# Where the heads of the last two slots and of the half slots are made in a graph layer with routed experts

## The chip, the cores and the metric

The kernel runs on one core of a Trainium2 chip. The metric is the device time of one execution in microseconds; the median of three runs before the change is 528.12 us. A core has a matrix engine (PE, with its weight loads shown apart as PEld), a vector engine (DVE), a scalar engine (ACT), a general engine (POOL, which here issues all indirect transfers) and a queue that issues plain transfers (SP).

## What is computed

The input is a table x of 2048 nodes with 256 features. The first half adds to each row a weighted sum of normalised neighbour rows over 67,584 edges. The second half, in which the change lies, is a layer of eight experts of which every row uses its two best:

```python
x = x + _L0_gnn_ref(_layernorm(x, axis=-1), edge_weight, edge_index, node_vec1)
x = x + _L0_ffn_ref(_layernorm(x, axis=-1)[None], ...)[0]
...
weights = top_p / top_p.sum(axis=-1, keepdims=True)
h = gelu(einsum('end,edh->enh', xe, W1) + b1)
y = einsum('enh,ehd->end', h, W2) + b2
out = (weights[:, :, None] * sel).sum(axis=1)
```

D is 256, the hidden width H is 1024, and all arithmetic here is in 32-bit floats.

## The kernel before

Only rows that chose an expert are computed for it. The rows of an expert are cut into **slots**: a whole slot has two tiles of 128 rows, a half slot has one (an expert with an odd number of tiles has one half slot). Which expert a slot belongs to, and which rows it holds, is known only on the chip. With this data 16 whole slots and 2 half slots run: `whole[0]` to `whole[13]`, two more whole slots set aside as `finals`, and `halves[0]` and `halves[1]`. Of them `whole[0]` to `whole[9]` and `finals` exist for any data; `whole[10]` on and all of `halves` stand in nested branches on the two counts `n_whole` and `n_half` (lines 1053 to 1063). A queue that finds a branch not taken goes through its other arm, where POOL waits for its outstanding transfers.

A slot has these steps:

- `load_slot` (L859) finds the slot's row numbers on DVE (L865 to L871, which end by writing the tile `to_i`), issues four loads on SP (scale columns `ec` L843, first weights L844, second weights L845, bias row `b` L846), and gathers the slot's rows `xs` with one indirect transfer per tile on POOL (L850).
- `head` (L876) transposes the rows on PE into the PSUM tile `px` (L883, four transposes for a whole slot, two for a half), scales them into `xeT` on DVE (L892), finds the rows' routing weights on DVE (L902 to L905) and multiplies the bias row by them on ACT (L907, one instruction per tile). `px` has one buffer.
- `layer_1` (L909) runs eight chunks `c`: two products on PE into `ph` (L918; the records count each as two) and a Gelu on ACT (L920). `ph` has three buffers. It has an argument `between` that runs a function ahead of chunk `c`.
- `layer_2` (L924) runs eight products per tile into `py` (L932, two buffers), and DVE makes `ys` (L935).
- `put_y` (L939) adds `ys` to rows of a table in device memory, `y_d`, with an indirect transfer on POOL (L940).

The order on PE, DVE, ACT and SP is written out by hand; POOL's is left to a scheduler. `run_slot(s, nxt, *more)` issues `load_slot` for the slots in `more`, then layer 1 of `s`, then the head of `nxt`, then layer 2 of `s`. A whole slot is loaded two slots ahead, into one of three sets of buffers in turn. The finals and the first two half slots have sets of their own, so each is loaded beside another slot: `finals[0]` in slot 6, `finals[1]` in slot 7, `halves[0]` in slot 8, `halves[1]` in slot 9. The heads of `finals[0]`, `finals[1]` and `halves[0]` are made one after the other behind slot 9 (L1046):

```python
for u in range(3, SURE - 2):
    k = u - (SURE - 2) + len(extra)
    run_slot(whole[u], whole[u + 1], whole[u + 2], *(extra[k:k + 1] if k >= 0 else []))
for s in (*finals, halves[0]):
    head(s)
```

Half slot `u` makes the head of half slot `u + 1` and loads half slot `u + 2`; whether these will run is not known when they are issued. In this data `halves[1]` is the last one that runs, so the head of `halves[2]` and the loads of `halves[2]` and `halves[3]` are not used. `to_i` of `halves[3]` shares its buffer with that of `halves[0]`.

At the end (L1066 to L1075) four plain transfers copy `y_d` to `out` (L1069), the rows of `finals[0]` are gathered from `y_d` (L850, `y_rows`) and added to its bias (L1074), its results are written to `out` (L953), the rows of `finals[1]` are gathered from `out`, and its results are written last.

Of the kernel before, what the change touches and what calls it, by code (L numbers as in the profile page):

```python
# [1 line left out]

# [7 lines left out]
F32 = mybir.dt.float32  # L10
# [11 lines left out]
P = 128  # L22
# [4 lines left out]
def kernel(  # L27
# [31 lines left out]
    N, D = x.shape  # L59
# [18 lines left out]
    SURE = (2 * N // P - NE) // TT  # L78
# [20 lines left out]
    for q in range(4):  # L99
        s = slice(q * NB // 4, (q + 1) * NB // 4)  # L100
# [85 lines left out]
    at = find.tile([P, GQ], F32, name="at")  # L186
# [156 lines left out]
    with tc.manual_schedule(engines=ALL):  # L343
# [29 lines left out]
        for n in range(NH):  # L373
# [20 lines left out]
            g, k = divmod(n - 2 * CB - 1, 2 * CB)  # L394
# [99 lines left out]
    with tc.If(n_used < E):  # L494
# [11 lines left out]
        with tc.tile_pool(name="any", bufs=2) as anyp, tc.tile_pool(  # L506
            name="ps_any", bufs=2, space=PSUM
# [36 lines left out]
    slotp = right("slot", 2)  # L544
# [34 lines left out]
    whole = []  # L579
    for i in range(EARLY + NF):  # L580
        k = i - EARLY if i - EARLY < LAST else i - EARLY + 2
        if k < NF:
            whole.append(Slot(k if i >= EARLY else i, TT, i % len(sets), i % (AHEAD + 2), i % 2,
                              i < EARLY))
    finals = [Slot(LAST + i, TT, 3 + i, AHEAD + 2 + i, 2 + i) for i in range(2)]
    halves = [Slot(NF + i, 1, 5 + i if i < 2 else (i - 2) % 3, AHEAD + 4 + i % 3, 4 + i % 2)
              for i in range(NE)]
    with tc.manual_schedule(engines=ALL - {ET.Pool}):
# [133 lines left out]
        def list_rows(s):  # L722
            in_lo, in_hi = s["in"]
            n = s["n"] * 2
            for m in range(n):
                nc.tensor.matmul(listed[:, s["i"], :], in_lo[:, m, :], in_hi[:, m, :],
                                 start=(m == 0), stop=(m == n - 1))
# [131 lines left out]
        def load_slot(s):  # L859

            e = ds(offs[s.i], 1)
            tk = slotp.tile([P, TT], F32, name="tk")
            for t in range(s.n):
                pick = slotp.tile([P, P], F32, name="pick", bufs=1)
                nc.vector.scalar_tensor_tensor(pick, iota_p, tile_0[:, t, s.i:s.i + 1], lists,  # L865
                                               op0=OP.is_equal, op1=OP.mult,
                                               accum_out=tk[:, t:t + 1])
            to = slotp.tile([P, TT], F32, name="to")
            nc.vector.scalar_tensor_tensor(to[:, :s.n], tk[:, :s.n], 0.5, spare_r[:, :s.n],
                                           op0=OP.is_lt, op1=OP.mult)  # L870
            nc.vector.scalar_tensor_tensor(tos[s.to][:, :s.n], tk[:, :s.n], -1.0, to[:, :s.n],  # L871
                                           op0=OP.add, op1=OP.max)
            get_weights(s, W1[e], cols_d[e], W2[e], b2[e])
            get_rows(s)

        def head(s):  # L876


            xs = sets[s.set][0]
            pt = ps_x.tile([P, KD, TS], F32, name="px")  # L880
            for t in range(s.n):
                for k in range(KD):
                    nc.tensor.transpose(pt[:, k, t * P:(t + 1) * P],  # L883
                                        xs[:, t, k * P:(k + 1) * P], ident)
            scale_rows(s, pt)
            set_weights(s)

        def scale_rows(s, pt):
            ec = sets[s.set][3]
            xeT = heads[s.head][0]  # L890
            for k in range(KD):
                nc.vector.tensor_scalar(xeT[:, k, :], pt[:, k, :s.n * P], ec[:, KH + k:KH + k + 1],  # L892
                                        ec[:, KH + KD + k:KH + KD + k + 1],
                                        op0=OP.mult, op1=OP.add)

        def set_weights(s):

            xs, w1, w2, ec, b2r = sets[s.set]
            xeT, wt, b2w = heads[s.head]
            expert = (iota_p if s.early else slot_e)[:, s.i:s.i + 1]  # L900
            mine = slotp.tile([P, TT, 2], F32, name="mine")[:, :s.n, :]
            nc.vector.tensor_scalar(mine, xs[:, :s.n, D:D + 2], expert, None, op0=OP.is_equal)  # L902
            wr = slotp.tile([P, TT, 2], F32, name="wr")[:, :s.n, :]
            nc.vector.tensor_mul(wr, mine, xs[:, :s.n, D + 2:D + 4])
            nc.vector.tensor_reduce(wt, wr, AX.X, OP.add)  # L905
            for t in range(s.n):
                nc.scalar.activation(b2w[:, t, :], b2r, AF.Copy, scale=wt[:, t:t + 1])  # L907

        def layer_1(s, between={}):  # L909
            xs, w1, w2, ec, b2r = sets[s.set]  # L910
            xeT = heads[s.head][0]
            hT = slotp.tile([P, KH, TS], F32, name="hT")
            for c in range(KH):
                if c in between:
                    between[c]()
                ph = ps_h.tile([P, TS], F32, name="ph")[:, :s.n * P]
                for k in range(KD):
                    nc.tensor.matmul(ph, w1[:, k, c * P:(c + 1) * P], xeT[:, k, :],  # L918
                                     start=(k == 0), stop=(k == KD - 1))
                nc.scalar.activation(hT[:, c, :s.n * P], ph, AF.Gelu, bias=ec[:, c:c + 1],  # L920
                                     scale=1.0)
            return hT

        def layer_2(s, hT, put, between={}):  # L924
            w2 = sets[s.set][2]
            xeT, wt, b2w = heads[s.head]
            for t in range(s.n):
                if t in between:
                    between[t]()
                py = ps_y.tile([P, D], F32, name="py")  # L930
                for c in range(KH):
                    nc.tensor.matmul(py, hT[:, c, t * P:(t + 1) * P], w2[:, c, :],  # L932
                                     start=(c == 0), stop=(c == KH - 1))
                ys = slotp.tile([P, D], F32, name="ys")
                nc.vector.scalar_tensor_tensor(ys, py, wt[:, t:t + 1], b2w[:, t, :], op0=OP.mult,  # L935
                                               op1=OP.add)
                put(s, t, ys)
# [23 lines left out]
            tc.declare_no_dep(st.ins, group=f"last{s.i}", reason="rows are unique in a slot")  # L961
            tc.add_to_no_dep_group(f"last{s.i}", st.ins)

        def run_slot(s, nxt, *more):
            for m in more:
                load_slot(m)
            hT = layer_1(s)
            if nxt is not None:
                head(nxt)
            layer_2(s, hT, put_y)  # L970
# [38 lines left out]
        hT = layer_1(whole[0])  # L1009
# [8 lines left out]
        set_weights(whole[0])  # L1018
        head(whole[1])
        layer_2(whole[0], hT, put_y, {1: lambda: sum_counts(last_b)})  # L1020
        places(last_b)
        enlist(last_b)
        slots(last_b["all"])
        set_shares(last_b)
        hT = layer_1(whole[1], {4: lambda: list_rows(last_b)})
# [5 lines left out]
        load_slot(whole[EARLY])  # L1031
        head(whole[2])
        layer_2(whole[1], hT, put_y)
        run_slot(whole[2], whole[3], whole[4])
        route_s.close()
        more_w = ctx.enter_context(tc.tile_pool(name="more_w", bufs=1, reuse_waits="tile"))
# [4 lines left out]
        nc.vector.memset(y_rows[1], 0.0)  # L1041
        extra = [finals[0], finals[1], halves[0], halves[1]]
        for u in range(3, SURE - 2):
            k = u - (SURE - 2) + len(extra)
            run_slot(whole[u], whole[u + 1], whole[u + 2], *(extra[k:k + 1] if k >= 0 else []))
        for s in (*finals, halves[0]):  # L1046
            head(s)
    _, (n_whole, n_half) = nc.values_load_multi_w_load_instructions(
        slot_i[0:1, NU:NU + 2], min_val=0, max_val=NF,
        skip_runtime_bounds_check_because="the sums of the experts' slots",  # L1050
# [1 line left out]
    at = lambda ss, i: ss[i] if i < len(ss) else None  # L1052
    with ExitStack() as nest:  # L1053
        for u in range(SURE - 2, len(whole)):
            s = whole[u]
            nest.enter_context(tc.If(n_whole > s.i))
            with tc.manual_schedule(engines=ALL - {ET.Pool}):
                run_slot(s, at(whole, u + 1), *whole[u + 2:u + 3])
    with ExitStack() as nest:  # L1059
        for u, s in enumerate(halves):  # L1060
            nest.enter_context(tc.If(n_half > s.i - NF))
            with tc.manual_schedule(engines=ALL - {ET.Pool}):
                run_slot(s, at(halves, u + 1), *halves[u + 2:u + 3])


    with tc.manual_schedule(engines=ALL - {ET.Pool}):  # L1066
# [3 lines left out]
        for f, y, rows, n in zip(finals, y_rows, (y_d, out), (N + TS, N)):  # L1070
            get_rows(f, y, rows, n)
            hT = layer_1(f)
# [27 lines left out]
```

## Time and profile before

| What | Value |
|---|---|
| median of three runs | 528.12 us (527.67 to 530.58) |
| the profiled execution | 529.07 us, span 527.3 us |
| granted PE clock, mean over the span | 0.955 |
| busy: PE, DVE, ACT, POOL | 457.7, 283.6, 191.6, 156.6 us |
| a whole slot in the steady part | 14.25 us |
| first whole slot in a branch (`whole[10]`) begins | 408.61 us |
| first half slot begins | 467.94 us |
| `finals[0]` begins on PE | 489.49 us |

The span runs from the first to the last instruction, and 1.77 us of the execution's time lie outside it. In the timelines below a row is: start, duration, engine, line, operation, tile written and tiles read, count, and in brackets how long the engine had been idle and what released it. An arrow points from what is read to what is written. SPq and POOLq are the queues that issue transfers.

The share of PE is high over the whole span, but the first 260 us (the graph part and the routing) are not touched by the change. The slots fill 260 to 520 us.

### The profile page before, as it was taken

What the parts mean: (1) busy time and instruction counts of PE and PEld (TensorE: products, weight loads), DVE (VectorE), ACT (ScalarE), POOL (GpSimd) and SP (SyncE); (2) the same over time, 40 slices, a digit from 0 to 9 for tenths busy, and PEclk for the clock granted to TensorE, in tenths of its full rate; (3) what the DMA queues carried; (4) which work ended last, traced back from release to release, by engine and by line L of the source; (5) the groups of instructions that cost most, each with busy time, mean ns of one, the idle gap of its engine ahead of it and who ended that gap; (6) DMA issues with size and microseconds to landing.
All of it is one profiled execution on the core that took longest, in us unless ns stands there. A gap on an engine that the chain in (4) does not pass through costs nothing. (4 is left out here: it accounts for less than half of the span.)

```text
span 527.3 us, 12108 instructions
## 1 busy us (share of the span) xinstructions
PE 457.7 (87%) x4998; PEld 393.3 (75%) x4998; DVE 283.6 (54%) x599; ACT 191.6 (36%) x439; POOL 156.6 (30%) x127
## 2 busy tenths in 40 slices
PE   0154889898899999899999999999997999996992
PEld 0043778687688788688887888888886888885881
DVE  5698989899999898217847222232234222221011
ACT  1424877333242412038382333333332333332220
POOL 2504153450603000000242533455443144422222
PEclk9995778999899999999999999999999899998997
DMA  6215776757567468894523996679999567748421
GB/s 205 71 42 146 217 222 217 211 174 247 177 205 216 138 187 234 273 347 156 178 50 82 325 341 180 188 234 356 365 363 360 165 178 193 205 102 284 118 106 39
DMA packets 87604, 106.75 MB, mean 202 GB/s; under 512 B 8640, under 2 KB 77360, under 8 KB 85424
## 3 DMA queue, kind: packets, MB, share of 16 engines
q1 hardware_dynamic: 78032, 90.73, 53.2%
q0 software_dynamic: 8032, 14.04, 11.4%
q10 hardware_dynamic: 1472, 1.06, 0.6%
q8 instruction: 44, 0.72, 0.5%
q14 instruction: 24, 0.20, 0.1%
HBM read 79.78 MB, written 28.14 MB: 205 GB/s over the span
## 5 line engine op out<-in xcount | busy, mean ns | idle before, releaser
L333 PE MATMUL py<-xn_sb,ac 128*128 128x264 f32 x512 | 122.5, 395 | 4.4 <-DMA ac<-ad 2.6
L918 PE MATMUL ph<-xeT,w 128*128 128x256 f32 (+1 forms) x576 | 122.5, 371 | 1.6 <-DVEq L1053 0.7
L932 PE MATMUL py<-w,hT 128*128 128x256 f32 x544 | 121.8, 382 | 0.0
L918 PEld LDWEIGHTS ph<-xeT,w 128*128 128x128 f32 x576 | 105.3, 192 | 16.1 <-issue 2.0
L333 PEld LDWEIGHTS py<-xn_sb,ac 128*128 128x128 f32 x512 | 96.1, 192 | 23.9 <-issue 2.9
L920 ACT ACTIVATE hT<-ph,ec 128x256 f32<-128x256 f32 (+1 forms) x144 | 66.5, 462 | 128.3 <-PE ph L918 75.5
L932 PEld LDWEIGHTS py<-w,hT 128*128 128x128 f32 x544 | 103.0, 192 | 13.5
L940 POOL DMA_INDIRECT y_d<-ys,to_i x30 | 48.9, 1630 | 110.2 <-DVE ys L935 88.7
L292 DVE TENSOR_TENSOR hl<-k,iota_b 128x4096 bf16<-128x4096 bf16 x32 | 73.1, 2285 | 3.4 <-PE pa L319 3.4
L319 PE MATMUL pa<-hl,hr 128*32 128x128 bf16 x3072 | 58.3, 241 | 18.3 <-DVE hr L299 15.9
L319 PEld LDWEIGHTS <-hr 128*32 128x32 bf16 x3072 | 52.0, 108 | 27.2 <-DVE hr L299 17.3
L850 POOL DMA_INDIRECT xs<-xr_d,to_i x40 | 41.7, 1043 | 73.7 <-DVE r L616 43.6
L299 DVE TENSOR_TENSOR hr<-eq,w 128x3072 bf16<-128x3072 bf16 x32 | 56.3, 1758 | 2.0 <-DVE eq L295 0.5
L892 DVE TENSOR_SCALAR xeT<-px,ec 128x256 f32<-128x256 f32 (+1 forms) x40 | 19.1, 519 | 70.6 <-PE px L883 68.6
L935 DVE SCALAR_TENSOR_TENSOR ys<-py,wt,b2w 128x256 f32<-128x256 f32 x34 | 16.3, 483 | 71.8 <-PE py L932 62.2
L322 ACT COPY ar<-pa 128x512 f32<-128x512 f32 x64 | 35.4, 583 | 39.6 <-PE pa L319 35.9
L221 POOL DMA_INDIRECT win_s<-in_src,at_i x8 | 13.7, 1709 | 92.7 <-DVE r L282 88.4
L338 DVE TENSOR_TENSOR acc<-acc,py 128x528 f32<-128x528 f32 x32 | 22.2, 700 | 23.0 <-PE py L333 23.0
L907 ACT ACTIVATE b2w<-b,wt 128x256 f32<-128x256 f32 x37 | 16.8, 500 | 39.6 <-DVE wt L905 36.5
L265 PE MATMUL pk<-ident,f 128*128 128x128 f32 x16 | 4.7, 348 | 20.7 <-DVE f L256 16.1
L295 DVE TENSOR_TENSOR eq<-k,iota_b 128x1024 bf16<-128x1024 bf16 x32 | 21.9, 684 | 0.0
L265 PEld LDWEIGHTS pk<-ident,f 128*128 128x128 f32 x16 | 2.4, 159 | 22.9 <-issue 13.0
(193 smaller groups left out, 312.7 us busy)
## 6 DMA issues: line engine op xcount, KB each, us to landing
w<-in_L_ffn_W SPq DMA_DIRECT2D x44, 1024.0 KB, 9.3
ad<-ar SPq DMA_DIRECT2D x32, 512.0 KB, 4.6
ac<-ad SPq DMA_DIRECT2D x16, 1024.0 KB, 6.0
b<-in_L_ffn_b SPq DMA_DIRECT2D x22, 128.0 KB, 9.7
out<-y_d SPq DMA_DIRECT2D x4, 512.0 KB, 6.6
xr_d<-rec SPq DMA_DIRECT2D x1, 1300.0 KB, 6.7
y_d<-acc SPq DMA_DIRECT2D x1, 1280.0 KB, 6.0
acc<-in_x ACTq DMA_DIRECT2D x2, 512.0 KB, 6.0
```

The costliest lines, as they stand in the source:

```text
L292: nc.vector.tensor_tensor(hl.rearrange("p g (n t) -> p g n t", t=2), two(k2[:, 0], g, P), pair(P), OP.is_equal)
L295: nc.vector.tensor_tensor(eq.rearrange("p g (n t) -> p g n t", t=2), two(k2[:, 1], g, RK), pair(RK), OP.is_equal)
L299: nc.vector.tensor_tensor(hr.rearrange("p g i (n t) -> p (g i) n t", t=2), eq[:, :, None, :].to_broadcast([P, GH, 3, RK]), w[:, :, None, : ...
L319: nc.tensor.matmul(pa[j * RK:(j + 1) * RK, m, :], hr[:, g, i, :], hl[:, g, :], start=(i == 0), stop=(i == 2), tile_position=(0, j * RK))
L322: nc.scalar.copy(ar[:, m0:m0 + 4, :], pa)
L333: nc.tensor.matmul(pa[:, i, :DX], acs[g * CB + c][:, b + i, :], xn_sb[:, g * CB + c, :], start=(c == 0), stop=(c == CB - 1))
L338: nc.vector.tensor_add(acc[:, b:b + 2, :], acc[:, b:b + 2, :], pa[:, :, :DX])
L850: nc.gpsimd.indirect_dma_start(out=(sets[s.set][0] if into is None else into)[:, t, :], out_offset=None, in_=(xr_d if rows is None else ro ...
L918: nc.tensor.matmul(ph, w1[:, k, c * P:(c + 1) * P], xeT[:, k, :], start=(k == 0), stop=(k == KD - 1))
L920: nc.scalar.activation(hT[:, c, :s.n * P], ph, AF.Gelu, bias=ec[:, c:c + 1], scale=1.0)
L932: nc.tensor.matmul(py, hT[:, c, t * P:(t + 1) * P], w2[:, c, :], start=(c == 0), stop=(c == KH - 1))
L940: st = nc.gpsimd.indirect_dma_start(out=y_d[:, :], out_offset=bass.IndirectOffsetOnAxis(ap=tos[s.to][:, t:t + 1], axis=0), in_=ys, in_offs ...
```

## The change

```diff
-                ys = slotp.tile([P, D], F32, name="ys")
+                ys = slotp.tile([P, D], F32, name="ys", bufs=4)
...
-        def run_slot(s, nxt, *more):
+        def run_slot(s, nxt, *more, between={}):
             for m in more:
                 load_slot(m)
-            hT = layer_1(s)
+            hT = layer_1(s, between)
...
         for u in range(3, SURE - 2):
-            k = u - (SURE - 2) + len(extra)
-            run_slot(whole[u], whole[u + 1], whole[u + 2], *(extra[k:k + 1] if k >= 0 else []))
-        for s in (*finals, halves[0]):
-            head(s)
+            k = u - (SURE - 2) + len(extra) + 1
+            run_slot(whole[u], whole[u + 1], whole[u + 2], *(extra[k:k + 1] if k >= 0 else []),
+                     between={4: partial(head, extra[k - 1])} if k > 0 else {})
...
         for u, s in enumerate(halves):
             nest.enter_context(tc.If(n_half > s.i - NF))
             with tc.manual_schedule(engines=ALL - {ET.Pool}):
-                run_slot(s, at(halves, u + 1), *halves[u + 2:u + 3])
+                if u > 1:
+                    head(s)
+                run_slot(s, None, *halves[u + 2:u + 3])
```

In words: the four extra slots are each loaded one slot earlier (in slots 5 to 8), and their heads are made inside slots 6 to 9, ahead of chunk 4 of layer 1. `halves[1]` thus gets its head in slot 9 and no longer in `halves[0]`. No half slot makes the head of the next one; from `halves[2]` on, a half slot makes its own at its start, inside its branch. `ys` has four buffers for two, 1 KB per partition each.

More of the change, by code (lines that the diff above doesn't have):

```diff
@@ L1 @@
 from contextlib import ExitStack
+from functools import partial
 import concourse.bass as bass
```

## The prediction

> **What bounds the kernel now.** I read the chain of waits first. From 478 us to the end it runs through transfers, not through PE:
>
> ```profile
> 478.31 1.59 DMA y_d<-ys,to_i
> 479.90 6.59 issue
> ...
> 486.69 1.07 POOL xs L850
> 487.76 1.77 issue
> ...
> 489.76 5.36 DMA y_d<-ys,to_i
> ...
> 498.36 7.93 DMA out<-y_d
> ```
>
> The reader is to see the two additions to `y_d`: that of `halves[0]` at 478.31, that of `halves[1]` at 489.76. The copy to `out` and the rest follow the second one at fixed distances, so the end moves with it.
>
> Second, the timeline between the two, to learn why the second comes so late:
>
> ```profile
> 475.26 3.73 PE L918 MATMUL ph<-xeT,w 128*128 128x128 f32 x32
> 476.94 1.07 POOL L850 DMA_INDIRECT xs<-xr_d,to_i  x1 [7.22 <-DVE to L869]
> 478.31 1.59 POOL L940 DMA_INDIRECT y_d<-ys,to_i  x1 [0.30 <-issue]
> 483.68 0.69 PE L883 MATMUL px<-ident,xs 128*128 128x128 f32 x2 [4.68 <-DMA xs<-xr_d,to_i]
> 483.95 4.60 PEld L932 LDWEIGHTS py<-w,hT 128*128 128x128 f32 x16
> 485.74 0.16 DVE L871 SCALAR_TENSOR_TENSOR to_i<-tk,to 128x1 int32<-128x1 f32 x1 [8.95 <-DMA y_d<-ys,to_i]
> 486.69 1.07 POOL L850 DMA_INDIRECT xs<-xr_d,to_i  x1 [6.79 <-issue]
> 488.99 0.48 DVE L935 SCALAR_TENSOR_TENSOR ys<-py,wt,b2w 128x256 f32<-128x256 f32 x1 [1.89 <-PE py L932]
> ```
>
> Two waits stand here side by side. PE sits 4.68 us for the gathered rows of `halves[2]`, whose head nobody uses, and layer 2 of `halves[1]` waits behind it. DVE sits 8.95 us at the row numbers of `halves[3]` until the addition of `halves[0]` has landed. PE's wait ends last by little: POOL was free again at 487.76, `ys` came at 488.99.
>
> Third, the windows by slot, for PE further up (columns: window, its length, then busy time and count of PE, PEld, DVE, ACT, POOL, granted clock, DMA share, GB/s):
>
> ```profile
> 390.00:404.25 14.25, 14.25 (x69) 12.50 (x68) 3.96 (x17) 4.69 (x10) 6.33 (x5) 1.00 1.08 361
> 404.25:408.61 4.36, 1.69 (x11) 0.99 (x10) 3.88 (x13) 1.28 (x3) 1.59 (x1) 0.93 1.09 356
> 408.61:424.34 15.73, 15.73 (x68) 13.65 (x69) 3.82 (x17) 5.23 (x12) 3.74 (x3) 0.91 0.54 160
> 424.34:438.59 14.25, 14.25 (x69) 12.55 (x68) 3.36 (x13) 4.69 (x10) 5.34 (x4) 1.00 0.71 194
> ```
>
> The three heads behind slot 9 cost PE 4.36 us, and the slot behind them takes 15.73 for 14.25, with the clock at 0.91. In one-microsecond windows it is 0.50 from 409 to 411 and 1.00 from 412 on.
>
> [...] half clock behind the 4.36 us gap, and again at 484 to 486 behind the 4.68 us wait. [...] the ten transposes in the gap indeed didn't keep the clock up. [...] the additions here took 3.8 to 10.1 us to land (median 6.8)[...].
>
> **The change part by part.** All against the profiled execution (span 527.3, time 529.07 us).
>
> *Heads out of the gap.* Removed: 4.36 us of gap and 1.48 us of slow clock (15.73 − 14.25), together 5.84. The branch on `n_whole` now stands directly behind slot 9. Its cost on PE was hidden; between the last transposes' end (408.23) and the first product (408.61) lay 0.38 us. From below it is nothing, from above about 0.7 (the exit from that nest at 467.94 shows 0.68 us idle); I take 0.4.
>
> *Heads into layer 1.* Four transposes cost PE 0.44 us (slot 7: head at 368.41, next product at 368.85), two cost 0.22 (471.59 to 471.81). More weighs what follows them on ACT. In slot 7, from the transposes it takes 0.64 us to L892 and 3.15 us to the end of L907. Ahead of chunk 4 the transposes start at 4 × 0.864 = 3.46 us into the slot (0.864 is the Gelus' spacing), so L907 ends at 6.61 and the Gelu of chunk 4, queued behind it, at 7.09. Chunk 7 wants its `ph` buffer back at 3.46 + 0.44 + 3 × 0.864 = 6.50: with release it waits some 0.65 us. A whole head thus costs 1.09 us. For a half head (L907 ends about 2.2 us after the transposes, by 471.59 to 473.81) the Gelu of chunk 4 is done at about 6.15 and chunk 7 wants it at 6.27: 0.22 us only. Sum: 2 × 1.09 + 2 × 0.22 = 2.62. From below, without any wait, 1.32; from above, if the slack of the half heads goes too and both waits double, 4.1. The other engines hide it: DVE is busy 4 of 14.25 us per slot.
>
> *Loads one slot earlier.* Each is four SP issues, one or two gathers and the DVE steps; they move past `load_slot` of one whole slot on SP and past two additions on POOL. Nothing is added in total. The DMA engines were full (share 1.07) in slots 7 to 9; now slots 6 to 8 are. The gathers took up to 8.9 us to land and have over 12 now. The bias rows are the tightest: issued 3.05 to 4.89 us into a slot and 11.8 to 13.2 us in landing, they are there 16.3 to 16.8 us after that slot's start; L907 wants them at 14.25 + 5.70 = 19.95. Cost nothing, with 3.2 us to spare; each microsecond beyond would be paid on ACT, then on PE.
>
> *Sum on PE up to `halves[0]`*: 5.84 − 0.4 − 2.62 = 2.82 us earlier. The additions of `whole[13]` move by as much. POOL then waits for their landing before the gather at 476.94, so this gather and the addition of `halves[0]` move by 2.82 too; that `halves[0]` itself loses a head of 0.22 us is hidden by POOL.
>
> *The unused head.* PE's 4.68 us wait, two transposes and 1.2 us of slow clock (4.79 for 3.62 us of the same 16 products in `halves[0]`) go. Late next is DVE's wait: L871 stays ahead of L935 in DVE's queue, and behind it the gather of `halves[3]` stays ahead of the addition of `halves[1]` on POOL. That gather ends at 487.76, the addition could start 0.30 us later (as it does at 478.31), at 488.06; it started at 489.76. So only 1.70 us of the wait are won. PE ends `halves[1]` at about 479.5 and is no longer in the chain.
>
> *`ys` with four buffers.* The wait of 0.42 us for a `ys` buffer in `halves[0]` (PE ended at 475.43, `ys` started at 475.85) lies under POOL's wait: nothing. L871 now carries waits for additions of two slots earlier, 28 us old in the steady part: nothing. Other tiles move in memory; the one early instruction that gains a wait, an iota on POOL at 216.42, is read at 246.64: nothing.
>
> *The end.* PE's finals start 9 us earlier, but `finals[0]` needs the gathered `y_d` rows, and the last bias addition came at 516.60 for transfers, not for PE. PE then stands 1.4 us at `py` and ends `finals[1]` near 510, ahead of that addition near 512. The tail keeps its length.
>
> Sum: 2.82 + 1.70 = 4.52 us. The profiled execution would be 524.6 us; it stands 0.95 above the median of the runs, so on the median 528.12 − 4.5 = 523.6 us.
>
> **The rivals.** *More is won (521.6 us).* The addition of `halves[0]` took 7.3 us to land under the loads of unused half slots, that of `halves[1]` 3.9. If the former lands as fast as 5.3, the end gains 2 more. Against it: these loads are released by the same queues and move along.
>
> *The gain upstream is eaten (526.4 us).* If the in-slot heads and the branch cost as much as the gap did, only the 1.70 us are left. For it speaks that my 2.62 is built from spacings, and that DMA is full there; against it, that its upper end (4.1 + 0.7) is still below 5.84.
>
> *Slower (531.6 us).* Bias rows of the extra slots land after 19.95 us. Then L907 holds the Gelus of chunks 4 to 7, and PE stops in chunk 7. At 2 us too late in each of four slots this costs 8 us: 528.1 − 4.5 + 8. It decides from 3.2 us more than landing takes now, and outweighs the gain from about 4.4. Against it: order and amount on SP stay as they were.
>
> **How the numbers follow.** Forecast 0.60 (522 to 525), more won 0.12, eaten 0.18, slower 0.10. A measurement here tells apart about 0.5%, 2.6 us: faster means below 525.5. Faster: 0.58 + 0.12 + 0.04 = 0.74; same: 0.02 + 0.14 = 0.16; slower 0.10. The range goes from 521.2 (more won) to 527.0 (eaten).
>
> **What would show it.** Right: no gap behind slot 9, `whole[10]` at 14.25 us and full clock; slots 6 and 7 about 1.1 us longer, slots 8 and 9 about 0.2; `halves[0]` starting near 465.1; L871 of `halves[3]` still waiting for the addition of `halves[0]`, near 483; the addition of `halves[1]` 0.3 us behind a gather, near 485.2. Wrong: an idle ACT ahead of L907 put down to `b`, PE idle in chunk 7 for over 1 us, a slow clock inside slots 6 to 10, or a last addition that no longer follows L871.

## The result, and the profile after

The changed kernel takes 525.37 us in the median of 16 runs, against 530.56 us of the kernel before in 16 runs of the same comparison. The ratio is 0.9897 with a 95% interval of 0.9872 to 0.9922: 1.0% faster, which is 5.5 us (the two medians lie 5.2 apart). Executions more than 1.5% above the fastest of their kernel (one of these 16, at 530.02 us) are left out of all ratios. The profiled execution took 521.57 us, with a span of 519.8 us.

Spans of single executions mislead here. The graph part, which the change doesn't touch, takes up to 14 us more or less from one execution to the next: in the traces of this study slot 6 begins between 342.91 and 356.74 us. So I measure from the first product of slot 6 to the end of the span, and cut this stretch at the three points that the prediction used: the start of `halves[0]` on PE, the addition of `halves[0]` to `y_d`, and that of `halves[1]`.

| Kernel (one trace each) | slot 6 to `halves[0]` | to its addition | to the addition of `halves[1]` | to the end | sum |
|---|---|---|---|---|---|
| before | 120.69 | 10.37 | 11.45 | 37.54 | 180.05 |
| after | 117.58 | 10.15 | 10.25 | 36.44 | 174.42 |
| after, a second trace | 117.60 | 8.40 | 10.04 | 37.73 | 173.77 |

The sum is 5.6 and 6.3 us shorter, in keeping with the 5.5 us of the comparison. Four lines of the windows of after show the upper part (columns: window, its length, busy time and count of PE, PEld, DVE, ACT, POOL, granted clock, DMA share, GB/s): slot 6, slot 9, the slot behind it, and a stretch to which I come back.

```profile
345.38:360.77 15.39, 14.96 (x74) 12.85 (x73) 5.89 (x24) 5.28 (x12) 7.32 (x6) 1.00 1.06 356
390.64:405.11 14.47, 14.47 (x72) 12.71 (x71) 4.55 (x18) 4.99 (x11) 5.33 (x4) 1.00 0.82 270
405.11:419.37 14.26, 14.26 (x70) 12.56 (x69) 3.46 (x13) 4.70 (x10) 5.33 (x4) 1.00 0.70 194
...
477.25:481.35 4.10, 0.00 (x2) 0.03 (x1) 0.31 (x2) 0.00 (x0) 0.00 (x0) 0.95 0.95 281
```

The gap of 4.36 us behind slot 9 is gone; `whole[10]` begins at 405.11, at the very end of slot 9, and runs at a granted clock of 1.00. Slots 6 and 7 take 15.39 us each for 14.25, slots 8 and 9 take 14.47 and 14.48. The timeline of after (columns as before):

```profile
345.38 3.62 PE L919 MATMUL ph<-xeT,w 128*128 128x256 f32 x16
348.83 0.60 PE L884 MATMUL px<-ident,xs 128*128 128x128 f32 x4
349.26 2.75 PE L919 MATMUL ph<-xeT,w 128*128 128x256 f32 x12
352.45 1.13 PE L919 MATMUL ph<-xeT,w 128*128 128x256 f32 x4 [0.43 <-ACT hT L921]
...
471.73 1.08 POOL L851 DMA_INDIRECT xs<-xr_d,to_i  x1 [6.99 <-PE ph L919]
473.11 1.59 POOL L941 DMA_INDIRECT y_d<-ys,to_i  x1 [0.30 <-issue]
473.63 3.62 PE L933 MATMUL py<-w,hT 128*128 128x256 f32 x16
481.04 0.16 DVE L872 SCALAR_TENSOR_TENSOR to_i<-tk,to 128x1 int32<-128x1 f32 x1 [9.50 <-DMA y_d<-ys,to_i]
481.35 8.63 PE L919 MATMUL ph<-xeT,w 128*128 128x256 f32 x32 [4.10 <-PEq L1059]
481.99 1.07 POOL L851 DMA_INDIRECT xs<-xr_d,to_i  x1 [7.28 <-issue]
483.36 1.58 POOL L941 DMA_INDIRECT y_d<-ys,to_i  x1 [0.31 <-issue]
...
510.74 0.48 DVE L936 SCALAR_TENSOR_TENSOR ys<-py,wt,b2w 128x256 f32<-128x256 f32 x1 [0.36 <-PE py L933]
```

In slot 6 the reader is to see the four transposes ahead of chunk 4 and the one PE wait in chunk 7, put down to a Gelu. Between the two additions, at 473.11 and 483.36, PE's wait for rows is gone, and what is late next is the wait of DVE (L872) for the addition of `halves[0]`, with the unused gather behind it, as forecast. Two things weren't forecast: PE stands 4.10 us in front of `finals[0]`, put down to its own queue at the branch of L1059 (the last of the four windows above: PE idle, DMA share 0.95), and then runs `finals[0]` at half clock for a while (granted clock 0.50 from 481.35 to 484 us, 1.00 from 485 on; 8.63 us for 7.07). And at the end the last `ys` waits for PE, 0.36 us. The chain of waits of after says the same of the additions:

```profile
473.11 1.59 DMA y_d<-ys,to_i
474.70 7.08 issue
...
481.99 0.34 POOL xs L851
...
483.36 5.59 DMA y_d<-ys,to_i
...
491.34 7.73 DMA out<-y_d
```

### The profile page after: what moved, and what is told of

The parts are those of the page before. It is cut to its first block, busy times and chain, and to the rows that moved or that the text cites. A ratio compares the mean times of both kernels' runs of the same rounds, so it can differ in the third digit from the quotient of the medians.

```text
span 519.8 us, 12093 instructions
## 1 busy us (share of the span) xinstructions
PE 453.8 (87%) x4996; PEld 390.3 (75%) x4996; DVE 282.6 (54%) x594; ACT 190.7 (37%) x438; POOL 154.2 (30%) x127
## 5 line engine op out<-in xcount | busy, mean ns | idle before, releaser
L222 POOL DMA_INDIRECT win_s<-in_src,at_i x8 | 11.6, 1454 | 94.0 <-DVE r L283 89.8
```

## The experiments

Each run has one trace, cut in the same way as above:

| Kernel | slot 6 to `halves[0]` | to its addition | to that of `halves[1]` | to the end | sum | ratio to before |
|---|---|---|---|---|---|---|
| heads in the slots only | 117.36 | 10.78 | 13.11 | 36.74 | 177.99 | 0.9943 (0.9916 to 0.997) |
| unused head only | 120.56 | 11.23 | 10.48 | 36.67 | 178.94 | 0.9969 (0.9947 to 0.9992) |
| late bias | 116.18 | 11.24 | 9.88 | 36.73 | 174.03 | 0.9886 (0.9853 to 0.9918) |
| late bias, again | 116.18 | 11.39 | 10.21 | 36.59 | 174.37 | 0.9867 (0.9801 to 0.9933) |
| four row-number tiles | 117.58 | 11.09 | 8.32 | 38.20 | 175.19 | 0.9872 (0.9845 to 0.9899) |
| two `ys` | 117.62 | 11.30 | 9.81 | 37.63 | 176.36 | 0.9929 (0.9888 to 0.9969) |
| two `ys`, again | 117.56 | 8.15 | 10.40 | 37.18 | 173.29 | 0.996 (0.992 to 1.0001) |
| loads in own branch | 117.54 | 8.07 | 7.03 | 36.96 | 169.60 | 0.9807 (0.9726 to 0.9887) |
| that and late bias | 116.18 | 8.07 | 7.02 | 36.89 | 168.16 | 0.9772 (0.9704 to 0.984) |
| that and late bias, again | 116.18 | 8.07 | 7.02 | 36.99 | 168.26 | 0.98 (0.9731 to 0.9869) |

**The two parts of the change, each alone.** First the changed kernel without its part on half slots: `halves[1]` gets its head behind layer 1 of `halves[0]` again, and the head of `halves[2]` is made though nobody uses it.

```diff
-                      between={4: partial(head, extra[k - 1])} if k > 0 else {})
+                      between={4: partial(head, extra[k - 1])} if 0 < k < 4 else {})
...
-                 if u > 1:
-                     head(s)
-                 run_slot(s, None, *halves[u + 2:u + 3])
+                 run_slot(s, at(halves, u + 1), *halves[u + 2:u + 3])
```

> The change without its half-slot part: heads of the two finals and of halves[0] inside slots 6 to 8, loads one slot earlier, but halves[0] makes the head of halves[1] and halves[1] the unused head of halves[2], as before. Theory (two separate gains): slot 6 to the start of halves[0] takes 117.4 us (120.7 before, 117.6 after; one half head of 0.22 is missing); PE then waits some 4.7 us again for the rows of halves[2], and the addition of halves[1] comes 11 to 11.5 us behind that of halves[0] (10.25 after). In all 3.0 to 4.3 us faster than before. Rival (the gap behind slot 9 was hidden by transfers and only the unused head counted): within 1 us of before.

It is 3.0 us faster than before by the ratio (medians 529.36 and 526.56), and 2.1 us in the traces (180.05 − 177.99). Slot 6 to `halves[0]` took 117.36 us, as expected; the distance between the additions was not the expected 11 to 11.5 us but 13.11. The timeline of this kernel shows why:

```profile
479.96 0.69 PE L884 MATMUL px<-ident,xs 128*128 128x128 f32 x2 [5.54 <-DMA xs<-xr_d,to_i]
480.44 6.01 PE L933 MATMUL py<-w,hT 128*128 128x256 f32 x16
486.49 0.48 DVE L936 SCALAR_TENSOR_TENSOR ys<-py,wt,b2w 128x256 f32<-128x256 f32 x1 [3.18 <-PE py L933]
```

PE waits longer for the unused rows (5.54 us), and the half clock that follows (0.50 from 480 to 483 us) now covers most of layer 2 (6.01 us for 3.62), on which the addition waits.

Then the kernel before with only its unused heads taken away:

```diff
-                 run_slot(s, at(halves, u + 1), *halves[u + 2:u + 3])
+                 if u > 1:
+                     head(s)
+                 run_slot(s, halves[1] if u == 0 else None, *halves[u + 2:u + 3])
```

> The kernel before with only its unused heads taken out: halves[0] makes the head of halves[1], later half slots make their own. Theory: the gap behind slot 9 stays (slot 6 to halves[0] 120.7 us), and the addition of halves[1] follows that of halves[0] by some 10.2 us for 11.45, since the row numbers of halves[3] still wait for it to land; 1.2 to 2.3 us faster than before. Rival (PE's 4.7 us wait was worth its full length): 5 us faster.

The gain is 1.6 us by the ratio and 180.05 − 178.94 = 1.1 in the traces; the additions lie 10.48 us apart. PE stands 4.08 us at the branch here too and takes 8.74 us for layer 1 of `finals[0]` (mean clock 0.66 from 485 to 490 us), so this cost belongs to the taking away of PE's wait, not to the heads in the slots. The two parts alone give 3.0 + 1.6 = 4.6 us by their ratios, the whole 5.5: the difference is within the intervals.

**What a head in a slot is made of.** In the changed kernel the bias rows of the four extra heads are multiplied behind the eight Gelus of the slot instead of ahead of that of chunk 4.

```diff
+        def weigh_bias(s):
+            b2r = sets[s.set][4]
+            _, wt, b2w = heads[s.head]
...
-                      between={4: partial(head, extra[k - 1])} if k > 0 else {})
+                      between={4: partial(head, extra[k - 1], False)} if k > 0 else {},
+                      then=extra[k - 1] if k > 0 else None)
```

> The changed kernel with the bias rows of the in-slot head weighed on ACT behind the eight Gelus of layer 1 instead of between the fourth and fifth. Theory (ACT's queue holds up PE in chunk 7): slots 6 and 7 take 14.69 us each for 15.39, slots 8 and 9 stay at 14.47; 1.4 us faster than the changed kernel. Rival (PE waits for the px bank or for DVE): slots 6 and 7 stay at 15.39, same time.

Slots 6 and 7 took 14.69 us each, slots 8 and 9 14.47. So of the 1.14 us of a whole head 0.70 were the Gelu held up behind the bias rows (forecast 0.65), and 0.44 are the transposes (forecast 0.44). `halves[0]` begins 1.4 us earlier. But the time moved by less than its interval can tell, so I ran it again beside the changed kernel itself on one chip.

> The changed kernel with the bias rows of in-slot heads weighed behind the eight Gelus, again. Theory A (PE sets the time from slot 6 to the first half slot, and the additions move with it): slots 6 and 7 at 14.69 us, and the ratio 0.2 to 0.3% below the changed kernel. Rival B (the additions wait for landings that do not move): same slots, ratio equal to the changed kernel within 0.1%.

> The changed kernel itself, to stand beside the three others on one chip. Both theories: ratio to before about 0.990.

The ratios were 0.9867 and 0.9886 (0.9841 to 0.9932), 0.2% apart and far inside the intervals. The traces say where the 1.4 us went: from `halves[0]` to its addition it took 11.24 and 11.39 us, for 10.15 and 8.40 in the changed kernel. In this stretch POOL waits until the last addition of `whole[13]` has landed, which took 6.99 and 7.14 us here and 5.92 and 4.16 there; the stretch is 4.2 us longer than this landing in all ten traces of kernels that load unused half slots. How long the landing takes goes, over the same ten traces, with the moment at which SP issues the second weights of `halves[2]`, the first unused slot: 1.5 to 1.9 us after the start of `halves[0]` the addition took 6.5 to 7.1 us, at 2.1 us 5.9 to 6.2, and at 2.3 to 2.4 us 3.9 to 4.2. So it looks like a race between the addition and these loads. That it isn't the late bias rows as such is seen from the two traces of the kernel with two `ys` (below): one program, 7.13 us in one and 3.93 in the other. No run moved this issue alone.

**Who holds PE in front of the finals?** Either DVE, whose wait at L872 keeps `ys` of `halves[1]` and with it a PSUM buffer, or the branch itself. In the changed kernel the row numbers of the half slots got four tiles in turn instead of three, so that L872 waits for no addition.

```diff
-     tos = [wpool.tile([P, TT], I32, name=f"to_i{i}") for i in range(AHEAD + 7)]
+     tos = [wpool.tile([P, TT], I32, name=f"to_i{i}") for i in range(AHEAD + 8)]
...
-     halves = [Slot(NF + i, 1, 5 + i if i < 2 else (i - 2) % 3, AHEAD + 4 + i % 3, 4 + i % 2)
+     halves = [Slot(NF + i, 1, 5 + i if i < 2 else (i - 2) % 3, AHEAD + 4 + i % 4, 4 + i % 2)
```

> The changed kernel with four tiles of row numbers for the half slots for three, so that those of halves[3] need not wait for the addition of halves[0]. DVE is then free for ys of halves[1] at about 477.3 us on the scale of the changed kernel's trace (481.15 there), and POOL adds it at about 478 (483.36 there). PE's 4.1 us wait ahead of the finals ends together with DVE's wait in the changed kernel. Theory A (PE's branch is slow by itself, because weights for unused half slots fill the DMA engines): PE's finals still begin about 11 us after the start of halves[1]'s layer 1, at half clock, PE then ends last, and the time is within 1 us of the changed kernel. Theory B (PE's wait hangs on the transfer that DVE waits for): the finals begin about 8 us after that start, and the time falls by 3 to 4.5 us.

The timeline of this kernel:

```profile
474.82 0.48 DVE L936 SCALAR_TENSOR_TENSOR ys<-py,wt,b2w 128x256 f32<-128x256 f32 x1 [4.62 <-PE py L933]
478.68 10.12 PE L919 MATMUL ph<-xeT,w 128*128 128x256 f32 x32 [3.90 <-PEq L1059]
479.90 1.58 POOL L941 DMA_INDIRECT y_d<-ys,to_i  x1 [5.37 <-DMA y_d<-ys,to_i]
...
509.56 0.48 DVE L936 SCALAR_TENSOR_TENSOR ys<-py,wt,b2w 128x256 f32<-128x256 f32 x1 [2.93 <-PE py L933]
```

DVE no longer waits, `ys` is there at 474.82, and PE stands 3.90 us all the same: it is the branch. The addition of `halves[1]` gains less than it might, since POOL lets it wait for the landing of the one before in any case (5.37 us idle), and at the end the last `ys` waits 2.93 us for PE. By the ratios the time is within 1.3 us of the changed kernel: behind DVE's wait stood another one that is only 1.7 to 1.9 us shorter (additions 8.32 us apart for 10.04 and 10.25), and the longer end takes part of that back.

**The loads of half slots that don't run.** In the changed kernel a half slot from `halves[2]` on is loaded at the start of its own branch, so that nothing is loaded for a slot that doesn't run. (With data that needs a third half slot, that slot would wait for its own loads; this wasn't tried.)

```diff
                  if u > 1:
+                     load_slot(s)
                      head(s)
-                 run_slot(s, None, *halves[u + 2:u + 3])
+                 run_slot(s, None)
```

> The changed kernel in which half slots from the third on are loaded inside their own branch, so that nothing is loaded for half slots that do not run. The DMA engines are then nearly idle during the two half slots. T is the start of halves[0] on PE. Theory (PE's wait ahead of the finals is its branch, made slow by the unused loads; the addition of halves[1] waits for that of halves[0] to land): PE's finals begin about T + 15 us at full clock (T + 18.4 in the changed kernel), the additions start near T + 8.2 and T + 15.2 (10.2 and 20.4 there), PE ends last, and the time is 3.5 to 5 us under the changed kernel, ratio to before about 0.981. Rival (the wait is a fixed price of leaving the nest): the finals begin at T + 18 us or later at half clock, and the time falls by 1 us at most.

The ratio is 0.9807; its interval just reaches that of the changed kernel, but the stretch from slot 6 on is 4.2 to 4.8 us shorter than in the two traces of the changed kernel. The timeline of this kernel:

```profile
473.61 1.57 POOL L941 DMA_INDIRECT y_d<-ys,to_i  x1 [6.29 <-DVE ys L936]
480.64 1.55 POOL L941 DMA_INDIRECT y_d<-ys,to_i  x1 [5.46 <-DVEq L1059]
481.09 7.14 PE L919 MATMUL ph<-xeT,w 128*128 128x256 f32 x32 [1.26 <-PEq L1059]
```

Each addition now follows its own `ys`, 7.03 us apart; PE stands 1.26 us at the branch instead of 4.10 and keeps its clock (1.00 from 480 to 485 us). The landings show what the unused loads had cost: the addition of `halves[0]` took 7.3 to 8.1 us to land in all ten traces of kernels that issue these loads, and 3.8 to 3.9 us in the three of kernels that don't (from the start of the addition to its semaphore).

How long the branches of L1059 took is seen in the view by line (columns: queue, operation, count, shortest/median/longest in ns, first and last start), first of after:

```profile
L1059 PEldq COMPARE_BRANCH  x4: 65/132/6528, 462.7 to 481.0; - x4
```

then of the kernel with the loads in their branch, and of the one with the heads in the slots only:

```profile
L1059 PEldq COMPARE_BRANCH  x4: 65/132/3688, 465.3 to 480.7; - x4
...
L1059 PEldq COMPARE_BRANCH  x4: 65/127/3487, 463.1 to 486.6; - x4
```

Three of the four are short in each; the one that leaves the nest takes 6.5, 3.7 and 3.5 us. The third kernel issues the unused loads as well, so the loads alone don't make the branch long. The packets of the DMA queues tell more. The trace marks some of them as "instruction", and those of one queue, q8, are 16 KB each. In after two of them lie inside the long branch (474.25 to 480.78): they start at 475.56 and 478.19. In the other two kernels only one lies inside, and the one ahead of it is there before PE comes to the branch. With the loads in their branch it starts 9.2 us after `halves[0]`, in after 12.6 us, beside other transfers (DMA share 1.04 from 474.96 to 476.96 us); PE comes to the branch at 11.3 us in both. In the kernel with the heads in the slots only it starts late too, at 12.3 us, but PE waits for rows first and comes to the branch at 16.7. So I read the long branch as PE meeting a packet there that the unused loads have held up; no run held it up alone. PE's instructions are the same in after and in the kernel with the loads in their branch. Three things go with these loads: the transfers, DVE's wait at L872 and POOL's unused gather. The four row-number tiles took DVE's wait away alone and brought the additions from 10.25 and 10.04 us apart to 8.32; without all three it is 7.03, and the first addition comes 0.3 and 2.1 us earlier as well.

**Both together.** Loads in their own branch and late bias rows:

> The kernel of the run before with the bias rows of in-slot heads weighed behind the Gelus as well. If the two are separate, 1.4 us less than that run, ratio to before about 0.978; if the end is set by transfers and not by PE's slots, the same as that run.

> Late bias rows and loads of the half slots in their own branches. Theory A (unused loads lengthen the landings and PE's branch): 1.0 to 1.3% below the changed kernel, ratio to before about 0.978. Rival B (the ratio of 0.977 measured earlier came from that chip): equal to the changed kernel within 0.4%.

The ratios are 0.9772 and 0.98, the second beside 0.9886 of the changed kernel on the same chip: 0.9% below it, somewhat less than the 1.0 to 1.3 expected, and with intervals that overlap a little. The stretch from slot 6 on is 5.5 to 6.3 us shorter than in the two traces of the changed kernel. This is the fastest version of the study. That it beats the kernel before, the ratios show; that it beats the changed kernel, the ratios and the traces together. Here the 1.4 us of the late bias rows do arrive: 168.16 and 168.26 against 169.60.

**Two buffers for `ys`.** In the changed kernel, `bufs=4` of `ys` was taken back:

```diff
-                ys = slotp.tile([P, D], F32, name="ys", bufs=4)
+                ys = slotp.tile([P, D], F32, name="ys")
```

> The changed kernel with two ys buffers as before. Theory (the wait for a ys buffer lies under POOL's wait): slot lengths and the distances between the two additions as in the changed kernel (15.39, 15.39, 14.47, 14.48; 10.2 us), time within 1 us of it. Rival (the buffers carry part of the gain): half the gain is gone, 2.5 us over the changed kernel.

> The changed kernel with two ys buffers again. Theory A (the wait for a ys buffer lies under the landing that POOL waits for in any case): within 0.3% of the changed kernel in this comparison. Rival B (the wait for ys is part of the gain): 0.4% or more slower than the changed kernel.

The first ratio, 0.9929, fell between the two theories. In the second comparison it was 0.996 beside 0.9886, on the rival's side, though the intervals overlap. The traces show no place for a loss: 173.29 us from slot 6 on in one, 176.36 in the other, where the addition of `halves[0]` came 11.30 us after its start; and slots 0 to 5 take 88.0 us with two buffers as in after. Whether the two more buffers are part of the gain stays open.

## Why the prediction was right, point by point

Forecast were 4.5 us (523.6 for 528.12); measured were 5.5 (1.03% for 0.85%). The absolute time, 525.37, lies 1.8 us above the forecast, because the three runs from which it started had a low median: in 16 runs the kernel before takes 530.56. The mechanism was right in each step that decides the time, and the sizes of these steps were off by half a microsecond or less; one step beside them, the finals on PE, was wrong in its reason.

How near the sum comes is in part luck. The second addition was to come 137.99 us after the start of slot 6; it came after 137.98 us in one trace of after, where errors of −0.29, −0.22 and +0.50 us cancel, and after 136.04 in the other. What the traces gain beyond 4.5 us lies in stretches for which no gain was forecast: in one trace the end (1.10 us), in the other the way from `halves[0]` to its addition (1.97 us). Both differ as much between the two traces of one kernel, and of the kernel before there is one trace only.

- *Heads out of the gap, 5.84 us.* Right. Gap and slow clock are gone. The branch behind slot 9, for which I took 0.4, cost nothing: `whole[10]` begins where slot 9 ends.
- *Heads into layer 1, 2.62 us.* Measured 15.39 + 15.39 + 14.47 + 14.48 − 4 × 14.25 = 2.73. The split into transposes and a held Gelu was confirmed by the late bias rows (0.44 and 0.70 for 0.44 and 0.65). PE, which sets the time here, gained 120.69 − 117.58 = 3.11 us for 2.82.
- *Loads one slot earlier, nothing.* Right: slots 6 to 9 are fully explained by the heads. In one trace of after the idle ACT ahead of a bias row of slot 9 is put down to `b`, which was named as a sign of being wrong; but it is the usual 1.57 us, and the slot is no longer for it.
- *The unused head, 1.70 us.* The step that was off: the additions came 1.20 and 1.41 us closer. That DVE's wait and the gather of `halves[3]` would be late next, and the addition 0.31 us behind that gather, was right. What was mis-sized is the landing between them: from the addition to the end of DVE's wait I used 7.43 us, as before; it took 7.93 us in after (473.11 to 481.04) and 7.72 in the second trace.
- *`ys` with four buffers, nothing.* Not settled: the traces show nothing, the ratios leave room for 0.3 to 0.7%.
- *PE no longer in the chain, finals ready near 510.* Wrong in its reason. I had PE start the finals behind `halves[1]` at once, 9 us earlier than before; counted from slot 6 they start 6.3 and 6.6 us earlier. Taking its wait for rows away laid bare a branch of 4.10 us and left the half clock in place, now in `finals[0]`. What the trace of before shows behind its gaps of 4.36 and 4.68 us came behind this one as well: 4.10 us idle, then a granted clock of 0.50 until 484 us (8.63 us for 7.07). The prediction didn't ask what its own new gap would do. This cost little: the last `ys` waits for it 0.36 us in one trace of after and 2.06 in the other.
- *The tail keeps its length.* 37.54 before, 36.44 and 37.73 after. The two traces of one kernel differ by more than the 1.10 us between before and after, so I put none of it down to the change.

Of the rivals, the one in which more is won came nearest: it had the addition of `halves[0]` land in 5.3 us for 7.3. In after it didn't (7.8 and 7.6 us), so what was won beyond the forecast wasn't won there. These loads do matter, though: without them the landing takes 3.8 us, and together with DVE's wait, the unused gather and the shorter branch 4.2 to 4.8 us are won.

## What to carry to other kernels

Ask of a wait that is removed not only which wait is late next on the path, but also what the engine that no longer waits will meet: here PE met a branch that had been hidden under its old wait, and a new idle stretch of 4.10 us, with a clock of 0.50 behind it. Work that is issued for something that may not run need not be free: here the DMA share between 465 and 480 us was 0.91 to 1.07 with it (after) and 0.01 to 0.38 without it (loads in own branch), and the addition of `halves[0]` took 7.3 us and more to land for 3.8. And when one part of a kernel varies by more than the effect, measure from a point behind it.

## What the runs showed of the hardware

The branches out of a nest were long on PE. Of its eleven compare-and-branches in each of the 13 traces, nine took 65 to 247 ns; the two that leave a nest, that of the whole slots and that of the half slots, took 3.4 to 6.8 us. In all 26 cases 16 KB packets marked "instruction" on queue q8 lie inside the branch: where there is one, the branch took 3.4 to 3.9 us, where there are two, 5.9 to 6.8. Two there are only at the exit from the half slots, in all eight traces of kernels that issue the unused loads and in which PE doesn't wait for rows first. Of the long branch PE stood 3.5 to 4.4 us with two packets. With one it stood 1.2 to 1.3 us at this exit in the kernels without the unused loads, and 0.5 to 0.7 us where it had more work in its queue: at the exit from the whole slots (in after 4.0 us of products ran on beside the branch) and at the exit from the half slots in the two kernels in which PE waits for rows first (in before 5.2 us; with the loads in their branch it was 2.9). That the branch waits for these packets is my estimate from these times; no run moved the packets alone.

Two indirect additions landed later in the kernels with the unused loads. The addition of `halves[0]`, 128 rows, took 7.3 to 8.1 us in ten traces with the unused loads and 3.8 to 3.9 us in three without. The one ahead of it, the last of `whole[13]`, took 3.9 to 7.1 us in the ten and 3.8 to 3.9 in the three. With 4.2 us added it gives the stretch from `halves[0]` to its addition in each of the ten (8.15 to 11.39 us); in the three this stretch is 8.07 us each time, since there PE's `ys` comes last and not the landing.
